# A selective scan on one core: the carried states copied by DMA instead of GpSimd, with three buffers for the scan's output

## The chip, the cores and the metric

The kernel runs on one core of one Trainium2 chip. The metric is the device time of one execution in microseconds. The core's engines are TensorE (PE, with its weight loads shown apart as PEld), VectorE (DVE), ScalarE (ACT), GpSimd (POOL) and SyncE (SP, which here issues nearly all DMAs); sixteen DMA engines move data.

## The reference

Four residual layers on an image batch of 8 × 64 × 64 × 192 in float32, each `x = x + layer(groupnorm(x))`. Layer 0 is a chunked state space block with an MLP, layers 2 and 3 are depthwise convolutions. The change lies in layer 1, a two-dimensional selective scan: the image is read in K = 4 orders (rows, columns, and both backwards), and in each order a recurrence runs over L = 4096 positions for 384 channels with 16 states each:

```
def step(h, inp):
    u_l, d_l, B_l, C_l = inp
    dA = jnp.exp(d_l[..., None] * A)
    dBu = d_l[..., None] * B_l[:, :, None, :] * u_l[..., None]
    h = dA * h + dBu
    y = jnp.sum(h * C_l[:, :, None, :], axis=-1)
    return (h, y)
inputs = (xs, delta, Bs, Cs)          # position first
h0 = jnp.zeros((Bn, 4, Din, N), xs.dtype)
_, ys = jax.lax.scan(step, h0, inputs)
```

Here `delta` is a softplus of a small projection of the input. The four results are put back in image order, added, normalised, gated and projected.

## The kernel before

The program runs layer 0, then layer 1 in three parts (`layer1_in`, `layer1_scan`, `layer1_out`), then layers 2 and 3. The scan part is the long one, and the change is in it.

**Tiling.** The positions lie along the free dimension, 512 (NJ) at a time; the 384 channels are three tiles (o = 0, 1, 2) of 128 partitions. A *piece* is one image b, one order k and one stretch p of 512 positions; there are 8 × 4 × 8 = 256 pieces, listed in `steps`. A piece has 16 states n; one state of one piece is a *group* g of three scans, one for each o. So there are 256 × 16 = 4096 groups and 12,288 scans, numbered j. The pieces of one image and order follow one another, and each needs the last value of every state of the piece before it: these values are kept in the small tile `st` [128 channels, 3, 16 states].

**One scan.** `ahead(j)` computes on ACT `dA = exp(dl * A)` (L1045) and on PE, into a PSUM tile `pd`, the term `delta * u * B` turned to channels by positions (L1051 and L1053). What PE turns is prepared on ACT by `scale` (L1029): for even groups a diagonal matrix `bd` of B, for odd groups the rows `sb` already multiplied. `scan(j)` runs the recurrence on DVE in one instruction (L1086), from `dA`, `pd` and the start value `st[:, o, n]`, into `h`. A tile `h` [128, 3, 512] serves all three scans of a group. GpSimd multiplies `h` by the row C, spread over all partitions in the tile `bc`, giving `hc` (L1095). After the third scan of a group GpSimd copies the last column of `h` (the first one for the backward orders) into `st[:, :, n]` (L1097), for the next piece. `behind(j)` adds `hc`, turned, into the PSUM tile `yt` on PE (L984), summing over the states. When a piece is done, ACT copies `yt` out to `ys` (L999) and SP stores it (L1003).

**Work for the next piece.** `prepare` returns a list of small steps with due times, done between the scans of the present piece: loads of `xt` and `dut` (L923, L925), a turn on PE (L930) and its copy `xs` on ACT (L934), the store of the C rows to DRAM, `bcd` (L936), three projections on PE (L943), the softplus on ACT (L948, L951, L954) and DVE (L957, `dl`), and the four products `dut` on DVE (L970). For k = 0 a further input `uD` is loaded (L1077).

**Order.** The order on PE, DVE, ACT and GpSimd is that in which the program is written (`every_engine`); each engine works strictly in order. The loop at L1111 calls, for each j: `fetch(g + 2)` at o = 0 (the DMA of `bc`, L1035), `ahead(j + 2)`, `scale(g + 2)`, `scan(j)`, `behind(j - 2)`, then the steps that are due. The DMAs on SP are ordered by the framework, and SP too works in order: a DMA that has to wait for an engine holds up the ones behind it. The buffers are `h` 2, `hc` 6, `dA` 5, `pd` 3, `bc` 4, `bd` 10, `sb` 8; a buffer is used again when all its readers are done.

Of the kernel before, what the change touches and what calls it, by code (L numbers as in the profile page):

```python
# [19 lines left out]
DP, DT = 128, 3  # L20
# [5 lines left out]
NJ = 512  # L26
# [3 lines left out]
class Names:  # L30
    n = 0


def mk(pool, shape, tag, **kw):
    Names.n += 1
    return pool.tile(shape, F32, tag=tag, name=f"{tag}_{Names.n}", **kw)
# [837 lines left out]
def layer1_scan(ctx: ExitStack, tc, a, load, ur, ut, xd, yk, cst):  # L874

    nc = tc.nc
# [16 lines left out]
    sp = ctx.enter_context(tc.tile_pool(name="s1", bufs=2))  # L893
# [120 lines left out]
    brows, decay, turned, states, held, outs, sts = {}, {}, {}, {}, {}, {}, {}  # L1014
# [54 lines left out]
    def scan(j):  # L1069
        if not 0 <= j < total:  # L1070
            return
        g, o = divmod(j, DT)
        s, n = divmod(g, N1)
        b, k, p, first = steps[s]
        if k == 0 and n == 5:
            v = ready[s]["u", o] = mk(sp, [DP, NJ], "uD", bufs=DT)
            nc.sync.dma_start(v, ur[b][:, o, p * NJ : (p + 1) * NJ])  # L1077
        if first and n == 0 and o == 0:
            sts[k] = mk(pp, [DP, DT, N1], "st")
        st = sts[k]  # L1080
        rev = slice(None, None, -1) if k >= 2 else slice(None)
        last = 0 if k >= 2 else NJ - 1
        if o == 0:
            states["h"] = mk(sp, [DP, DT, NJ], "h", bufs=2)
        h = states["h"]
        nc.vector.tensor_tensor_scan(  # L1086
            h[:, o, rev],
            decay.pop(j)[:, rev],
            turned.pop(j)[:, rev],
            0.0 if first else st[:, o, n : n + 1],  # L1090
            ALU.mult,
            ALU.add,
        )
        hc = states[j] = mk(sp, [DP, NJ], "hc", bufs=6)
        nc.gpsimd.tensor_tensor(hc, h[:, o, :], held[g], ALU.mult)  # L1095
        if o == DT - 1:
            nc.gpsimd.tensor_copy(st[:, :, n], h[:, :, last])  # L1097

    with every_engine(tc):
        for _, f, *v in prepare(*steps[0][:3], ready[0]):  # L1100
            f(*v)
            if f.__name__ == "turned_xd":
                tc.keep_in_program_order(nc.scalar.preload_act_table_set("natural_log_exp_and_others"))
        fetch(0)
        fetch(1)
        scale(0, range(NB))
        scale(1, range(NB))
        ahead(0)
        ahead(1)
        todo, late = [], []  # L1110
        for j in range(total + 3):  # L1111
            g, o = divmod(j, DT)
            s, i = divmod(j, PER)
            if i == 5 and s + 1 < len(steps):
                todo = prepare(*steps[s + 1][:3], ready[s + 1])
            if o == 0:
                fetch(g + 2)
            ahead(j + 2)
            scale(g + 2, ((0, 1), (2,), (3,))[o])
            while late:  # L1120
                f, *v = late.pop(0)
                f(*v)
            scan(j)
            behind(j - 2)
            while todo and todo[0][0] <= i - 5:
                _, f, *v = todo.pop(0)
                f(*v)
# [190 lines left out]
```

## Time and profile before

| | |
|---|---|
| Runs (three) | 26157.72, 26190.96, 26194.59 us; median 26190.96 |
| Profiled execution, own time | 26178.77 us |
| Its span, first to last instruction | 26177.0 us |
| Busy over the span | PE 23676.9 (90%), PEld 18442.5 (70%), DVE 22201.3 (85%), ACT 20110.8 (77%), POOL 17658.9 (67%) |
| Mean granted TensorE clock | 0.948 over the span, 1.00 in the scan from 14500 to 19500 us |
| DMA, whole span | 1461962 packets, 2275.55 MB, mean 87 GB/s |

The profile is one execution of the program. An engine is busy from an instruction's start to its end; instructions of one engine can overlap, so the sum of durations can be more than the busy time, and starts show the pace better than durations. In the groups of instructions, `hc<-h,bc` means that the tile `hc` is written from `h` and `bc`; then follow the shapes, the count, the busy time with the mean in nanoseconds, and the idle time of the engine just before these instructions, with the one that ended most of it. In the waits, three numbers stand behind a pair: microseconds in total, times, longest. In a timeline the columns are start, duration and engine, instructions of one kind in a row are merged (x3), and what is in brackets is the idle time before, with its releaser. In a line of a stretch, the two first numbers are its bounds, the next its length, then come the busy times of PE, PEld, DVE, ACT and POOL with the counts, the clock, the DMA engines' busy share and GB/s.

### The profile page before, as it was taken

What the parts mean: (1) busy time and instruction counts of PE and PEld (TensorE: products, weight loads), DVE (VectorE), ACT (ScalarE), POOL (GpSimd) and SP (SyncE); (2) the same over time, 40 slices, a digit from 0 to 9 for tenths busy, and PEclk for the clock granted to TensorE, in tenths of its full rate; (3) what the DMA queues carried; (4) which work ended last, traced back from release to release, by engine and by line L of the source; (5) the groups of instructions that cost most, each with busy time, mean ns of one, the idle gap of its engine ahead of it and who ended that gap; (6) DMA issues with size and microseconds to landing.
All of it is one profiled execution on the core that took longest, in us unless ns stands there. A gap on an engine that the chain in (4) does not pass through costs nothing.

```text
span 26177.0 us, 442405 instructions
## 1 busy us (share of the span) xinstructions
PE 23676.9 (90%) x156160; PEld 18442.5 (70%) x156160; DVE 22201.3 (85%) x25001; ACT 20110.8 (77%) x40019; POOL 17658.9 (67%) x18396
## 2 busy tenths in 40 slices
PE   7888888888899999999999999999999999987766
PEld 4444444445588888888888888888888888863322
DVE  6777777756799999999999999999999999986566
ACT  4555555544499999999999999999999999974322
POOL 2222222210199999999999999999999999972100
PEclk8888888889999999999999999999999999998878
DMA  1111111113333333333333333333333333346311
GB/s 56 42 43 42 44 41 44 35 40 115 112 101 94 97 102 94 96 103 94 96 103 94 96 102 95 95 101 96 95 100 97 95 99 97 96 143 198 120 34 29
DMA packets 1461962, 2275.55 MB, mean 87 GB/s; under 512 B 247181, under 2 KB 773133, under 8 KB 1458202
## 3 DMA queue, kind: packets, MB, share of 16 engines
q1 hardware_dynamic: 1445402, 2196.90, 28.9%
q0 software_dynamic: 14336, 50.34, 0.5%
q8 instruction: 1232, 20.19, 0.3%
q14 instruction: 992, 8.13, 0.1%
HBM read 1811.37 MB, written 435.42 MB: 86 GB/s over the span
## 4 chain that ended last, share of the span: by engine, by line
PE 37%; ACT 29%; POOL 13%; DVE 13%; issue 6%; DMA 2%; POOLq 0%; SPq 0%; DVEq 0%; ACTq 0%
ACT dA L1045 12%; POOL hc L1095 10%; PE pd L1051 6%; ACT sb L1029 6%; PE yt L984 5%; DVE h L1086 5%; ACT bd L1029 4%; PE y L643 3%; PE fc L677 3%; DVE x L71 2%; PE pd L1053 2%; DMA yin<-y 2%; PE mm L399 2%; PE mm L943 2%; PE y L576 1%
## 5 line engine op out<-in xcount | busy, mean ns | idle before, releaser
L1095 POOL TENSOR_TENSOR hc<-h,bc 128x512 f32<-128x512 f32 x12288 | 15443.8, 1291 | 477.5 <-DVE h L1086 337.3
L1086 DVE TENSOR_TENSOR_SCAN h<-dA,st,pd 128x512 f32<-128x512 f32 x10752 | 12951.9, 1262 | 533.1 <-PE pd L1051 371.8
L1045 ACT ACTIVATE dA<-dl,A_logs 128x512 f32<-128x512 f32 x12288 | 8785.3, 715 | 46.9 <-DVE h L1086 39.6
L984 PE MATMUL yt<-sq,hc 128*128 128x128 f32 x49152 | 7489.9, 275 | 203.2 <-POOL hc L1095 102.8
L1051 PE MATMUL pd<-bd,dut 128*128 128x128 f32 x49152 | 6581.5, 277 | 254.2 <-DVE h L1086 232.1
L1051 PEld LDWEIGHTS pd<-bd,dut 128*128 128x128 f32 x49152 | 5968.6, 192 | 610.1 <-PE yt L984 342.9
L984 PEld LDWEIGHTS yt<-sq,hc 128*128 128x128 f32 x49152 | 5668.5, 141 | 649.3 <-POOL hc L1095 629.2
L1029 ACT ACTIVATE sb<-dut,xt 128x384 f32<-128x384 f32 x8192 | 4762.6, 606 | 1.1 <-DVE dut L970 1.0
L1053 PE MATMUL pd<-sq,sb 128*128 128x128 f32 x24576 | 3739.6, 275 | 9.3 <-DVE h L1086 0.4
L1053 PEld LDWEIGHTS pd<-sq,sb 128*128 128x128 f32 x24576 | 2821.8, 141 | 480.5 <-DVE dl L957 380.8
L1029 ACT ACTIVATE bd<-sq,xt 128x128 f32<-128x128 f32 x8192 | 3010.2, 392 | 0.0
L1086 DVE TENSOR_TENSOR_SCAN h<-dA,pd 128x512 f32<-128x512 f32 x1536 | 1772.8, 1203 | 115.4 <-PE pd L1051 75.8
L71 DVE SCALAR_TENSOR_TENSOR x<-x,w,x 96x3969 f32<-96x3969 f32 (+1 forms) x192 | 838.3, 4366 | 486.9 <-ACT x L64 483.9
L538 POOL TENSOR_TENSOR xdt<-xb,dtv 128x384 f32<-128x384 f32 x256 | 222.2, 868 | 1366.9 <-ACT xb L532 1366.8
L413 POOL COPY halo<-raw 128x12 f32<-128x12 f32 x64 | 13.0, 202 | 1375.7 <-ACT raw L403 1375.7
L304 DVE SCALAR_TENSOR_TENSOR x<-xs,cpe_w,x 96x504 f32<-96x504 f32 (+1 forms) x1024 | 902.1, 881 | 30.1 <-ACT x L292 20.3
L826 DVE SCALAR_TENSOR_TENSOR u<-xa,conv_w,u 128x504 f32<-128x504 f32 x1152 | 850.0, 742 | 50.2 <-ACT u L818 12.5
L943 PE MATMUL mm<-xs,w_dt 13*128 13x512 f32 x1536 | 863.0, 641 | 1.8 <-DVE dl L957 1.0
L677 PE MATMUL fc<-ff,fc_w 128*96 128x512 f32 x1536 | 861.0, 677 | 2.7 <-DVE xo L680 2.7
L1097 POOL COPY st<-h 128x3 f32<-128x3 f32 x4096 | 831.1, 203 | 0.0
L304 DVE SCALAR_TENSOR_TENSOR xs<-x0h,cpe_w,xs 96x504 f32<-96x504 f32 (+1 forms) x1024 | 757.8, 745 | 23.7 <-ACT xs L292 2.5
L643 PE MATMUL y<-hn,fc_w 96*128 96x512 f32 x1536 | 750.2, 627 | 0.1
(234 smaller groups left out, 25752.7 us busy)
## 6 DMA issues: line engine op xcount, KB each, us to landing
bc<-bcd SPq DMA_DIRECT2D x4096, 256.0 KB
yin<-y SPq DMA_DIRECT2D x256, 768.0 KB
csb<-csd SPq DMA_DIRECT2D x256, 384.0 KB
dut<-ut SPq DMA_DIRECT2D x128, 768.0 KB
y<-ys SPq DMA_DIRECT2D x128, 768.0 KB
dut<-ut SPq DMA_DIRECT2D x256, 384.0 KB
y<-ys SPq DMA_DIRECT2D x256, 384.0 KB
xt<-x1d SPq DMA_DIRECT2D x128, 384.0 KB
```

The lines of the kernel that those rows point to most:

```text
L71: nc.vector.scalar_tensor_tensor(d[:, h0:h1, w0:w1], s[:, h0 + dy : h1 + dy, w0 + dx : w1 + dx], w[:, ct, tap : tap + 1], d[:, h0:h1, w0:w ...
L304: nc.vector.scalar_tensor_tensor(d[:, :, w0:w1], s[:, dy : dy + R, w0 + dx : w1 + dx], w[:, ct, tap : tap + 1], d[:, :, w0:w1], ALU.mult, ...
L643: nc.tensor.matmul(ps, f1w[:, ct, o * 128 : (o + 1) * 128], hn2[q][:, ct, :], start=ct == 0, stop=ct == CT - 1)
L677: nc.tensor.matmul(ps, f2w[:, o, ct * CP : (ct + 1) * CP], ff[:, o, :], start=o == 0, stop=o == 5)
L943: nc.tensor.matmul(ps, w_dt[:, k, o * 128 : (o + 1) * 128], made["xs"][0 : 1 + R1, :], start=True, stop=True)
L984: nc.tensor.matmul(yt[:, t * 128 : (t + 1) * 128], src[:, t * 128 : (t + 1) * 128], mat, is_transpose=mat is ident, start=first and t == 0 ...
L1029: nc.scalar.activation(v, src, AF.Copy, scale=m["xt"][:, t, 1 + R1 + n : 2 + R1 + n])
L1045: nc.scalar.activation(dA, ready[s]["dl"][:, o, :], AF.Exp, scale=aneg[:, k, o, n : n + 1])
L1051: nc.tensor.matmul(dst, ready[s]["dut"][:, t, cols], brows[g, t], start=True, stop=True)
L1053: nc.tensor.transpose(dst, brows[g, t][:, cols], ident)
L1086: nc.vector.tensor_tensor_scan(h[:, o, rev], decay.pop(j)[:, rev], turned.pop(j)[:, rev], 0.0 if first else st[:, o, n : n + 1], ALU.mult, ...
L1095: nc.gpsimd.tensor_tensor(hc, h[:, o, :], held[g], ALU.mult)
```

## The change

The copy of the last column into `st` on GpSimd becomes a DMA issued by SP. It moves one float from each of three columns in each of 128 partitions, so 384 single floats, within SBUF. The tile `h` gets three buffers in place of two. On PE, DVE and ACT the instructions and their order stay the same; GpSimd's list loses the 4096 copies; SP's list gains 4096 DMAs, each ahead of the `bc` fetch for four groups later. The first scan of a group waited, for the `h` buffer, for work of GpSimd two groups back; it now waits for work of GpSimd and for the state DMA of the group three back.

```
@@ def scan(j)
         rev = slice(None, None, -1) if k >= 2 else slice(None)
         last = 0 if k >= 2 else NJ - 1
         if o == 0:
-            states["h"] = mk(sp, [DP, DT, NJ], "h", bufs=2)
+            states["h"] = mk(sp, [DP, DT, NJ], "h", bufs=3)
         h = states["h"]
...
         hc = states[j] = mk(sp, [DP, NJ], "hc", bufs=6)
         nc.gpsimd.tensor_tensor(hc, h[:, o, :], held[g], ALU.mult)
         if o == DT - 1:
-            nc.gpsimd.tensor_copy(st[:, :, n], h[:, :, last])
+            nc.sync.dma_start(st[:, :, n : n + 1], h[:, :, last : last + 1])
```

More of the change, by code (lines that the diff above doesn't have):

```diff
@@ L1083, in scan @@
         if o == 0:
-            states["h"] = mk(sp, [DP, DT, NJ], "h", bufs=2)
+            states["h"] = mk(sp, [DP, DT, NJ], "h", bufs=3)
         h = states["h"]
@@ L1096, in scan @@
         if o == DT - 1:
-            nc.gpsimd.tensor_copy(st[:, :, n], h[:, :, last])
+            nc.sync.dma_start(st[:, :, n : n + 1], h[:, :, last : last + 1])
     with every_engine(tc):
```

## The prediction

> **What bounds the kernel now.** I read the page first (busy times, costliest groups), then the busy times of one 5 ms stretch of the scan, its waits, and the timelines of single engines over one piece.
>
> The page gives the size of what is removed. In the groups (busy us, mean ns; then idle before), the state copy L1097 is a short POOL instruction that follows every third L1095:
>
> ```profile
> L1095 POOL TENSOR_TENSOR hc<-h,bc 128x512 f32<-128x512 f32 x12288 | 15443.8, 1291 | 477.5 <-DVE h L1086 337.3
> ...
> L1097 POOL COPY st<-h 128x3 f32<-128x3 f32 x4096 | 831.1, 203 | 0.0
> ```
>
> The stretch 14500 to 19500 us shows no free engine: of 5000 us PE is busy 4857, DVE 4788, ACT 4883, POOL 4880, and the DMA engines 0.35.
>
> ```profile
> 14500.00:19500.00 5000.00, 4856.81 (x40097) 4425.50 (x40096) 4787.50 (x4344) 4883.23 (x9871) 4879.54 (x5053) 1.00 0.35 98
> ```
>
> A piece (16 states of three scans) takes 62.93 us there: the copies' times repeat at that distance. 5000/62.93 is 79.5 pieces, 1270 groups of three; 256 pieces are the whole stage. Idle per piece: ACT 1.47 us, POOL 1.52, PE 1.80, DVE 2.67.
>
> The waits of the same stretch say what that idle time is. ACT's is nearly all waits for PE (xs and ys); DVE waits for PE's pd; PE waits for POOL's hc; a scan hardly ever waits for POOL, so two h buffers are not short today:
>
> ```profile
> PEld yt L984 <- POOL hc L1095: 191.3, 552, 0.5
> DVE h L1086 <- PE pd L1051: 137.6, 186, 1.3
> ...
> ACT xs L934 <- PE mm L930: 51.7, 79, 0.9
> ACT ys L999 <- PE yt L984: 45.0, 72, 1.3
> ...
> ACT dA L1045 <- DVE h L1086: 10.9, 19, 0.6
> ...
> DVE h L1086 <- POOL hc L1095: 0.4, 1, 0.4
> ```
>
> The timelines show how these hang together. POOL, back to back:
>
> ```profile
> 15005.17 3.76 POOL L1095 TENSOR_TENSOR hc<-h,bc 128x512 f32<-128x512 f32 x3
> 15008.88 0.18 POOL L1097 COPY st<-h 128x3 f32<-128x3 f32 x1
> 15009.03 3.76 POOL L1095 TENSOR_TENSOR hc<-h,bc 128x512 f32<-128x512 f32 x3
> ```
>
> One group takes 3.86 us here (15005.17 to 15009.03; the trace's median is 3.84). Instructions overlap: by the trace's starts, one hc follows another after 1.237 us, and after 1.367 us where a copy lies between. So a copy costs POOL 0.130 us, not the 203 ns of its row. DVE without a stall:
>
> ```profile
> 15001.84 1.28 DVE L1086 TENSOR_TENSOR_SCAN h<-dA,st,pd 128x512 f32<-128x512 f32 x1 [0.26 <-PE pd L1051]
> 15004.32 3.78 DVE L1086 TENSOR_TENSOR_SCAN h<-dA,st,pd 128x512 f32<-128x512 f32 x3 [1.20 <-PE pd L1051]
> ...
> 15035.97 28.56 DVE L1086 TENSOR_TENSOR_SCAN h<-dA,st,pd 128x512 f32<-128x512 f32 x24
> ```
>
> Its starts lie 1.171 us apart, 3.51 per group. For the eight groups in which DVE has only scans, POOL thus falls 0.33 us per group behind it: the start of hc after the end of its scan grows from 0.14 us (group 14 of a piece) to 2.17 (group 5 of the next). PE works in order and takes hc as input, so it comes late too; then PE holds up DVE (0.26 and 1.20 us above, group 6) and ACT:
>
> ```profile
> 14998.62 0.58 ACT L934 COPY xs<-mm 45x512 f32<-45x512 f32 x1 [0.66 <-PE mm L930]
> ```
>
> In groups 6 to 13 ACT's softplus and DVE's dl and dut set the pace; POOL waits there and its backlog vanishes.
>
> **The change part by part.**
>
> *4096 copies leave POOL.* 4096 × 0.130 = 532 us of POOL's path. It isn't all gain. The next engine is ACT with 1.47 us idle per piece: 256 × 1.47 = 376 us is the ceiling as long as ACT does the same work (the change takes none from it). What can be had is ACT's waits that come from POOL's backlog. With copies gone POOL loses 3 × 1.237 − 3.51 = 0.20 us per group in place of 0.33; over the seven steps from group 14 to group 5 the lag ends at 0.14 + 7 × 0.20 = 1.54 in place of 2.17 or more, 0.63 us shorter. ACT's wait for xs falls in group 5 and is 51.7/79 = 0.65 us per piece: nearly all of it goes. Its wait for ys is 45.0/79 = 0.57, in groups 15 and 0, where the lag shrinks from 0.5–0.9 to 0.3–0.5: I take 0.2. Sum 0.85 us per piece, 256 × 0.85 = 218 us. Late next is ACT itself, then PE, which keeps its 0.57 − 0.2 of ys and its own matmuls between pd and yt.
>
> *4096 DMAs come onto SP's queue.* SP's issues in the trace take 0.32 us for 128 rows (bc) and 0.43 for 512 rows of 180 bytes (xt); I take 0.45 for 384 rows. With bc's 0.32 that is some 0.8 us per 3.9 us group, so SP has room. SP now stands at each of them until the third scan is done. Queued behind it: bc for four groups on, and once per piece bcd, xt, dut, y, uD. The order of instructions has bc(g+4) behind st(g); bc(g+4) waits for hc of group g, which itself starts after that scan, so the added wait delays no bc. The others have slack of 10 us and more (xt: issued at 15037.55, turned by PE at about 15061). I put all this at nothing; without that cover, a late bc would stop POOL, one for one.
>
> *The DMA's landing.* It reads h, so the buffer of h is free only when it has landed. By the order of the changed kernel's instructions the first scan of a group waits for the DMA of the group three before it. That is two groups, 7.0 us, after the third scan ended. Between st's issue at that end and the next use lie: 0.45 issue, about 1 us to the first packet (bc issued at 15001.30, first packet at 15002.25), its packets, and what is ahead in the rings (bc: 8 packets × 84 ns per engine = 0.7 us). That leaves 7.0 − 2.2 = 4.8 us for 24 packets per engine. This is what the third buffer pays for: with two, the time would be 3.5 us and the cover 1.3 us. For its own sake the third buffer is worth nothing (0.4 us of waits in 5000).
>
> *What 384 packets of four bytes cost* isn't in the trace of before: no DMA there moves single elements from SBUF to SBUF. The nearest rows: the 180-byte packets of xt take 15 ns each (median), the 24-byte ones of small loads 9 ns, and xt's 512 packets all ran between 15038.94 and 15040.28, 1.34 us. So 24 × 15 = 0.36 us per engine and group beside 0.35 × 3.96 = 1.39 us of other traffic, a share of about 0.45. Against it stands the Trainium skill, "DMA: Bandwidth & Descriptors": under "Rules for kernel authors" a strided last dimension becomes one descriptor per element and transfers under 64 KB are mostly overhead, and under "Measured (HBM→SBUF, 128 partitions, SWDGE, issued from GpSimd)" it counts about 10.5 ns per packet of the transfer, not of the engine. By that, 384 packets take an estimated 4.0 us, longer than a group, and with the other 1.39 the DMA engines would set 5.4 us per group: 1.46 × 4096 = 6 ms more. The row is from this chip's own queue and has 512 packets in 1.34 us, so I follow it: cost nothing, bounds 0 and +6 ms. It can't be below zero: the DMA takes nothing away but the copy, counted above.
>
> Sum against the profiled execution: its own time 26178.8 us (span 26177.0) − 218 = 25961; the median of the runs, 26191, is 12 us above it, so 25973. I say 25970.
>
> **The rivals.**
>
> *ACT's waits go altogether.* For: with POOL below DVE's stalls PE is earlier everywhere, and 107.6 of ACT's 116.8 idle us are waits for others. Gain 1.3 to 1.47 us per piece, 330 to 376 us: about 25840.
>
> *PE holds it where it is.* For: PE is busy 4857 of 5000, and DVE's stall of 1.20 us ends on pd right after a 1.12 us matmul (L943) in PE's own order, not on hc. Then xs and ys wait as before and the gain is at most 0.2 us per piece: 26140 to 26191. Against: PE's weight loads wait 191.3 us for hc in this stretch, the longest of all waits.
>
> *The state DMA lands late (the slower side).* Place: the first scan of a group, waiting for the DMA three groups back. It decides from a landing over 7.0 us after the third scan's end, that is from 4.8 us / 24 = 200 ns per packet in quiet stretches, and earlier in the 7 us of each piece in which xt, dut and y keep the DMA engines 50 to 80% busy. Two waits of half a microsecond per piece there: 256 × 1.0 = 256 us more, 26450. Against: 15 ns per packet in the nearest row. Beyond 107 ns per packet (24 × 107 ns + 1.39 = 3.96) the DMA engines are the bound in every group and it is far worse.
>
> **How the numbers follow.** 0.2% is 52 us, about what a measurement of this kernel can tell from no change. Forecast (25900 to 26080) 0.48; ACT's waits gone 0.17; PE holds it 0.15; late landing 0.20. Faster is the first two, 0.65; same is the third, 0.15; slower the last, 0.20. The range, 25830 to 26240, takes in the first three and the mild edge of the last.
>
> **What would show it.** L1097 gone from POOL, and hc's starts 1.237 us apart throughout; ACT's wait for xs from 0.65 to below 0.2 us per piece; DVE's stall in group 6 shorter; DMA share in the scan 0.40 to 0.50; a piece near 62.1 us. I am wrong if DVE's h shows waits for a DMA, if st's packets take far over 15 ns, or if ACT waits for PE as long as before though POOL is earlier.

## The result and the profile after

The changed kernel takes 25995.07 us (median of four runs, 25988.56 to 26014.83); the kernel before, run beside it, 26182.07. The ratio is 0.9931, with a 95% interval of [0.9914, 0.9948]: 187 us or 0.7% faster. The profiled execution took 25998.18 us, against 26178.77 before, which is 180.6 us less. The stage from the first scan to the last hc shrank by 180.1 us (16217.7 to 16037.5 in the traces), so all of it lies in the scan.

The page's groups. L1097 is gone from POOL. The idle time ahead of hc rose from 477.5 to 814.5 us: a part of what the copies gave back is now waiting.

```profile
L1095 POOL TENSOR_TENSOR hc<-h,bc 128x512 f32<-128x512 f32 x12288 | 15304.6, 1287 | 814.5 <-DVE h L1086 358.3
L1086 DVE TENSOR_TENSOR_SCAN h<-dA,st,pd 128x512 f32<-128x512 f32 x10752 | 12878.6, 1260 | 447.0 <-PE pd L1051 311.0
```

The stretch from 14500 to 19500 us (bounds, length, busy PE, PEld, DVE, ACT, POOL, clock, DMA share, GB/s). POOL falls from 4880 to 4770 busy us although it does 1% more hc; the other engines do more in the same 5 ms; the DMA share rises from 0.35 to 0.41:

```profile
14500.00:19500.00 5000.00, 4877.35 (x40551) 4476.67 (x40550) 4813.68 (x4388) 4930.62 (x9973) 4770.31 (x3831) 1.00 0.41 99
```

Its waits (us in total, times, longest):

```profile
PEld yt L984 <- POOL hc L1095: 119.1, 330, 0.4
DVE h L1086 <- PE pd L1051: 117.6, 120, 1.3
...
ACT ys L999 <- PE yt L984: 46.6, 73, 1.3
...
ACT dA L1045 <- DVE h L1086: 12.2, 21, 0.6
...
PE yt L984 <- POOL hc L1095: 4.0, 26, 0.2
...
ACT xs L934 <- PE mm L930: 1.2, 5, 0.3
```

For hc, PE has one line in the waits as PEld and one as PE; the second read, before:

```profile
PE yt L984 <- POOL hc L1095: 31.1, 133, 0.3
```

PE's waits for hc fell from 191.3 + 31.1 to 119.1 + 4.0, DVE's waits for L1051 from 137.6 to 117.6 us (186 to 120 times), ACT's wait for xs from 51.7 to 1.2. ACT's wait for ys stayed. DVE's scans wait for no DMA in this stretch. The timeline of DVE over one piece shows a part of what went: before, group 6 had two stalls, 0.26 and 1.20 us; now the first is gone and the second is as long as it was.

```profile
15011.11 29.44 DVE L1086 TENSOR_TENSOR_SCAN h<-dA,st,pd 128x512 f32<-128x512 f32 x25
15041.75 3.78 DVE L1086 TENSOR_TENSOR_SCAN h<-dA,st,pd 128x512 f32<-128x512 f32 x3 [1.20 <-PE pd L1051]
```

From the starts of hc in the traces one gets the pace by groups of a piece (means over k = 1 to 3, the last piece of each order left out; us), and the lag, which is hc's start after the end of its scan, at the last scan of group 5 (median):

| kernel | groups 14, 15, 0 to 6 | groups 7 to 13 | piece | lag |
|---|---|---|---|---|
| before | 34.57 | 28.27 | 62.84 | 2.23 |
| changed | 33.41 | 28.74 | 62.15 | 1.75 |

In nine groups POOL works without a pause and gains 1.16 us, which is 9 × 0.13. In the other seven it used to work off its lag; now it arrives earlier and waits there, and 0.47 us is given back. What is left is 0.69 us per piece, 177 us in 256 pieces.

The starts of DVE's scans tell where in the piece the time went (means over the same pieces). From the last scan of group 3 to the first of group 6, DVE took 9.01 us before and takes 8.35 now: 0.66 of the 0.69 us lies there, where POOL's lag is largest. The stall of 0.26 us is its largest part; the rest are gaps so short that the timeline merges them into its rows.

### The profile page after: what moved, and what is told of

Read it like the earlier page. It is cut to its first block, busy times and chain, and to the rows that moved or that the text cites. A ratio compares the mean times of both kernels' runs of the same rounds, so it can differ in the third digit from the quotient of the medians.

```text
span 25996.4 us, 448176 instructions
## 1 busy us (share of the span) xinstructions
PE 23556.4 (91%) x156160; PEld 18440.5 (71%) x156160; DVE 22125.1 (85%) x25001; ACT 20098.7 (77%) x40019; POOL 17143.5 (66%) x14300
## 2 busy tenths in 40 slices
DMA packets 3100407, 2282.47 MB, mean 88 GB/s; under 512 B 1885581, under 2 KB 2411533, under 8 KB 3096602
## 4 chain that ended last, share of the span: by engine, by line
ACT 42%; PE 38%; DVE 11%; POOL 3%; issue 3%; DMA 2%; SPq 0%; POOLq 0%; DVEq 0%; ACTq 0%
ACT dA L1045 18%; ACT sb L1029 10%; PE pd L1051 7%; PE yt L984 6%; ACT bd L1029 6%; DVE h L1086 3%; PE y L643 3%; PE fc L677 3%; DVE x L71 2%; DMA yin<-y 2%; PE mm L399 2%; PE pd L1053 2%; POOL hc L1095 2%; ACT ys L999 1%; PE y L576 1%
## 5 line engine op out<-in xcount | busy, mean ns | idle before, releaser
L1095 POOL TENSOR_TENSOR hc<-h,bc 128x512 f32<-128x512 f32 x12288 | 15304.6, 1287 | 814.5 <-DVE h L1086 358.3
L1051 PE MATMUL pd<-bd,dut 128*128 128x128 f32 x49152 | 6581.3, 277 | 253.5 <-DVE h L1086 231.3
L1051 PEld LDWEIGHTS pd<-bd,dut 128*128 128x128 f32 x49152 | 5968.4, 192 | 609.4 <-PE yt L984 342.2
```

What stands on the lines that cost most here:

```text
L1051: nc.tensor.matmul(dst, ready[s]["dut"][:, t, cols], brows[g, t], start=True, stop=True)
```

## The experiments

Ten kernels were run, in three sets on three chips: the first four, the next four, and the last two. Each set had the kernel before beside it on the same chip; ratios are to that kernel, with their 95% intervals, and kernels of different sets are compared by these ratios alone.

**Three buffers alone.** The kernel before with

```
-            states["h"] = mk(sp, [DP, DT, NJ], "h", bufs=2)
+            states["h"] = mk(sp, [DP, DT, NJ], "h", bufs=3)
```

> The kernel before with three buffers for h, the copies still on GpSimd. Theory (the gain is GpSimd's 0.130 us per group, which reaches the end through ACT's wait for xs): no change from before, 26160 to 26200 us, since scans waited for GpSimd only 0.4 us in 5 ms. Rival (the third buffer lets the scans run further ahead and gives part of the 187 us): 26000 to 26130.

Measured: 26192.18 us, ratio 1.0007 [0.9999, 1.0015]. The third buffer gives nothing by itself; the rival falls.

**The DMA with two buffers.** The changed kernel with `bufs=2` for h.

> The changed kernel with two buffers for h. Theory (the third buffer is the cover of the DMA's landing): in the changed kernel's trace the state DMA lands 2.3 us after its issue in the median and over 4.3 us in one case of ten, and one landing in five comes later than the first scan two groups on. So scans wait for the DMA, 0.5 to 2 us per piece after what GpSimd's backlog absorbs: 26120 to 26500, at or above the kernel before. Rival (landings are quick enough, the third buffer does nothing): 25980 to 26020.

Measured: 26426.32 us, ratio 1.0094 [1.0080, 1.0107]. So it is 0.9% slower than before, and 1.6% slower than with three buffers (1.0094/0.9931). In its waits over the same stretch DVE now waits for the DMA:

```profile
DVE h L1086 <- DMA st<-h: 82.9, 97, 2.6
DVE h L1086 <- PE pd L1051: 64.3, 126, 1.6
```

and its timeline shows one such wait, and one for POOL's hc, in the groups that ran without a gap in the changed kernel:

```profile
15014.37 7.13 DVE L1086 TENSOR_TENSOR_SCAN h<-dA,st,pd 128x512 f32<-128x512 f32 x6
15022.43 10.65 DVE L1086 TENSOR_TENSOR_SCAN h<-dA,st,pd 128x512 f32<-128x512 f32 x9 [0.93 <-DMA st<-h]
15033.78 11.82 DVE L1086 TENSOR_TENSOR_SCAN h<-dA,st,pd 128x512 f32<-128x512 f32 x10 [0.70 <-POOL hc L1095]
```

The third buffer is the cover of the DMA's landing; a piece takes 63.97 us without it (measured as in the table above).

**No state kept.** The changed kernel without the DMA:

```
         if first and n == 0 and o == 0:
             sts[k] = mk(pp, [DP, DT, N1], "st")
+            nc.gpsimd.memset(sts[k], 0.0)
...
-            nc.sync.dma_start(st[:, :, n : n + 1], h[:, :, last : last + 1])
+            pass
```

> The changed kernel without the state DMA: the last columns are not kept, st is set to zero once per image and order, and every piece after the first starts from zero. Three buffers for h. Theory (the DMA costs nothing): the same as the changed kernel, 25970 to 26010. Rival (the DMAs' packets, issues or landings cost part of what the copies gave back): 25800 to 25950.

Measured: 25993.79 us, ratio 0.9931 [0.9918, 0.9943], the changed kernel's own ratio. 4096 DMAs behind three buffers cost nothing that can be measured; the rival falls.

**ACT's xs copy one scan later.** The kernel before with

```
-        at = [(0, fetch_rows), (8, turn_xd), (9, turned_xd)]
+        at = [(0, fetch_rows), (8, turn_xd), (10, turned_xd)]
```

> The kernel before, with the copies on GpSimd and two h buffers; only the due time of ACT's copy of xs is 10 in place of 9, one scan later. Theory (the gain goes through ACT's wait for xs, 0.65 us per piece): that wait goes here too, and with it 0.4 to 0.65 us per piece, 100 to 166 us: 26010 to 26080. Rival (the wait is a symptom and GpSimd's own path sets the time of a piece): 26150 to 26200.

Measured: 26172.81 us, ratio 1.0002 [0.9993, 1.0010]. No gain, but the run doesn't decide: ACT's wait was not taken away, it went to the next thing that ACT wants from PE:

```profile
ACT e L948 <- PE mm L943: 67.4, 79, 1.1
ACT ys L999 <- PE yt L984: 45.0, 72, 1.3
```

My theory that the gain goes through ACT's wait for xs was now in doubt. I formed another: POOL's lag reaches the end through PE's order. `ahead(j + 2)` stands ahead of `behind(j - 2)` in each turn of the loop, so PE must turn hc(j − 5) before it makes the pd of scan j. As long as POOL's lag is below a limit PE finds hc ready; above it PE waits, and the next scans wait for PE. In the kernel before, POOL's lag would by my estimate grow to some 0.14 + 8 × 0.33 = 2.8 us in group 6, but the trace has it level off at 2.2: the rest, so the theory, is passed on to DVE.

**The DMA in the nine groups only.** The changed kernel with

```
         if o == DT - 1:
-            nc.sync.dma_start(st[:, :, n : n + 1], h[:, :, last : last + 1])
+            if 7 <= n <= 13:
+                nc.gpsimd.tensor_copy(st[:, :, n], h[:, :, last])
+            else:
+                nc.sync.dma_start(st[:, :, n : n + 1], h[:, :, last : last + 1])
```

> The changed kernel with the state DMA only in groups 14, 15 and 0 to 6 of a piece (9 of 16), where GpSimd falls behind the scans; in groups 7 to 13 GpSimd copies as before. Theory (only GpSimd's lag in those groups reaches the end, and only what it has over about 2.2 us): the whole gain, 25975 to 26015 us. Rival (every copy counts alike): 9/16 of 187 us, about 26077.

Measured: 26002.69 us, ratio 0.9932 [0.9920, 0.9945]: the whole gain, with 9 copies of 16 removed. DVE takes 8.36 us from the last scan of group 3 to the first of group 6, as in the changed kernel.

**The DMA in the other seven groups.** The same edit with the condition `not 7 <= n <= 13`.

> The counterpart: the state DMA in groups 7 to 13 (7 of 16), GpSimd's copies in groups 14, 15 and 0 to 6; three buffers for h. Theory (in groups 7 to 13 GpSimd waits for others anyway): no gain, 26160 to 26200 us. Rival (every copy counts alike): 7/16 of 187 us, about 26100.

Measured: 26190.40 us, ratio 1.0007 [0.9998, 1.0016]: nothing, although 1792 copies are gone and POOL's busy time in the stretch is 80 us below that of before:

```profile
14500.00:19500.00 5000.00, 4852.18 (x40056) 4421.09 (x40056) 4787.76 (x4340) 4879.50 (x9862) 4799.18 (x4496) 1.00 0.37 98
```

Copies don't count alike; where they stand decides. DVE's 9.01 us from group 3 to group 6 stay as they were, at 8.99.

**The softplus later.** The kernel before with

```
-        at = [(0, fetch_rows), (8, turn_xd), (9, turned_xd)]
+        at = [(0, fetch_rows), (8, turn_xd), (10, turned_xd)]
...
-            at += [(11 + 4 * o, step_mm, o), (12 + 4 * o, step_abs, o), (13 + 4 * o, step_exp, o)]
-            at += [(14 + 4 * o, step_ln, o), (16 + 4 * o, step_add, o)]
+            at += [(11 + 4 * o, step_mm, o), (14 + 4 * o, step_abs, o), (15 + 4 * o, step_exp, o)]
+            at += [(16 + 4 * o, step_ln, o), (18 + 4 * o, step_add, o)]
...
-            at += [(26 + 3 * t, turn, t), (27 + 3 * t, turned, t)]
+            at += [(28 + 3 * t, turn, t), (29 + 3 * t, turned, t)]
```

> The kernel before, copies on GpSimd and two h buffers, with the xs copy one scan later (10) and, other than with that copy alone, the softplus steps on ACT and DVE and the turns of dut two scans later each. With xs alone ACT's wait for PE only went over to the first softplus step (67.4 us in 5 ms in place of 51.7 at xs), so that run didn't take the wait away. Theory ACT (GpSimd's lag reaches the end through ACT's wait): no such wait is left, 26010 to 26080 us. Theory DVE (it reaches the end through PE's pd, for which the scans wait): 26150 to 26200, the waits of DVE for pd in groups 2 to 6 as before.

Measured: 26195.32 us, ratio 1.0009 [1.0000, 1.0018]. ACT no longer waits for PE at xs or at the softplus, yet nothing is gained; the wait came back at ys (115.5 us in place of 45.0). Theory ACT asked for 26010 to 26080 us and falls, as far as this run can tell. Theory DVE had the time right, but the waits for pd didn't stay as they were: some of them were now put down to ACT's dA:

```profile
ACT ys L999 <- PE yt L984: 115.5, 79, 1.7
DVE h L1086 <- ACT dA L1045: 94.4, 90, 1.3
DVE h L1086 <- PE pd L1053: 75.9, 147, 1.0
DVE h L1086 <- PE pd L1051: 44.6, 102, 1.2
```

So this run speaks against ACT, and alone it doesn't prove PE.

**ACT's ys copy later.** The changed kernel, the copies of yt taken one scan later (the loop runs one turn longer):

```
-            late.append((take, s, o, outs.pop((s, o))))
+            late.append((j + 4, take, s, o, outs.pop((s, o))))
...
-            while late:
-                f, *v = late.pop(0)
+            while late and late[0][0] <= j:
+                _, f, *v = late.pop(0)
```

> The changed kernel with ACT's copy of yt to ys one scan later, which leaves nothing out. ACT waits there for PE 46.6 us in 5 ms, 0.58 us per piece, the one wait of ACT that the prediction had taken for GpSimd's and that stayed. Theory (ACT's idle time is what bounds a piece): up to 0.58 us per piece, 148 us, 25850 to 25900. Rival (in groups 15 and 0 ACT has time to spare, since it runs ahead until its dA buffers are full): no change from the changed kernel, 25980 to 26010.

Measured: 26004.27 us, ratio 0.9934 [0.9921, 0.9946], as the changed kernel. ACT's wait went from ys back to xs:

```profile
ACT xs L934 <- PE mm L930: 51.3, 73, 1.2
...
ACT ys L999 <- PE yt L984: 8.2, 21, 0.4
```

The changed kernel with ACT's xs wait back at its old size is no slower. By these runs that wait is time which ACT has to spare, and it shows up wherever ACT first needs PE.

**PE turns hc later, copies kept.** The test of the new theory: the kernel before with (and the loop one turn longer)

```
-            behind(j - 2)
+            behind(j - 3)
```

> The kernel before, copies on GpSimd and two h buffers, with one edit: PE turns hc into yt one scan later in its order (three scans behind in place of two), so PE asks GpSimd for hc one scan of 1.17 us later. Nothing is left out. Theory (GpSimd's lag reaches the end where PE, in order, waits for hc ahead of the pd that the next scans need, from a lag of about 2.2 us on): the limit rises to about 3.3 us, the lag of 2.8 at the end of the nine groups stays below it, and the gain of the change, some 180 us, comes without touching the copies: 25900 to 26010. Rival (GpSimd's own time over a piece sets the pace, whatever PE does): 26150 to 26200.

Measured: 25978.73 us, ratio 0.9931 [0.9919, 0.9944]: a gain as large as the change's, with every copy still on GpSimd and two h buffers. In the timelines POOL is as slow as before, 3.84 us per group:

```profile
15001.25 3.79 POOL L1095 TENSOR_TENSOR hc<-h,bc 128x512 f32<-128x512 f32 x3
15004.94 0.23 POOL L1097 COPY st<-h 128x3 f32<-128x3 f32 x1
15005.09 3.80 POOL L1095 TENSOR_TENSOR hc<-h,bc 128x512 f32<-128x512 f32 x3
```

but PE hardly waits for it any more (PEld for hc 31.0 us in place of 191.3), and DVE's stalls in group 6 are 0.18 and 0.36 us in place of 0.26 and 1.20:

```profile
PEld yt L984 <- POOL hc L1095: 31.0, 108, 0.4
...
DVE h L1086 <- POOL st L1097: 16.2, 72, 0.4
```

```profile
15016.74 1.28 DVE L1086 TENSOR_TENSOR_SCAN h<-dA,st,pd 128x512 f32<-128x512 f32 x1 [0.18 <-POOL st L1097]
15018.39 3.82 DVE L1086 TENSOR_TENSOR_SCAN h<-dA,st,pd 128x512 f32<-128x512 f32 x3 [0.36 <-PE pd L1051]
```

The 0.18 is the wait for an h buffer: at this lag (2.54 us) the two buffers do become short, and they cost DVE 16.2 us of waits in the stretch.

That the sums agree is in part chance, since the two kernels don't gain in the same places. By the starts of the scans (k = 1 to 3), DVE's 9.01 us from the last scan of group 3 to the first of group 6, where the change saves 0.66, fall by 0.47 here, with POOL no faster. That is the theory's share. The stall of 1.20 us, which the change left alone, falls by 0.83 us, and 0.66 us is given back up to group 10. Pieces of k = 0 gain 1.26 us each (the change: 0.69) and those of k = 1 to 3 gain 0.59 (the change: 0.70), means over all of them.

**The same in the changed kernel.**

> The changed kernel (state DMA, three h buffers) with the same edit, PE turns hc one scan later. Theory (with the copies gone the lag is 1.8 us, already below the limit): little more, at most PE's last wait for hc in group 6, 0.31 us per piece or 80 us: 25900 to 26000, and within 0.3% of the kernel before with this edit. Rival (GpSimd's own time counts): the full difference between the two kernels stays, about 187 us.

Measured: 25962.73 us, ratio 0.9925 [0.9912, 0.9939], 16 us below the run before it. With PE's order loosened, the copies and the third buffer together are worth 16 us and not 187; which of the two brings the 16 wasn't tried, and by the starts of the scans they lie in the pieces of k = 0, while those of k = 1 to 3 take as long as in the run before. It is the fastest kernel of the study, though its interval overlaps that of the changed kernel. The table with four of these runs (k = 1 to 3, as above):

| kernel | groups 14, 15, 0 to 6 | groups 7 to 13 | piece | lag |
|---|---|---|---|---|
| DMA in the nine groups | 33.38 | 28.77 | 62.15 | 1.73 |
| DMA in the other seven | 34.53 | 28.37 | 62.90 | 2.23 |
| before, PE turns later | 34.55 | 27.70 | 62.25 | 2.54 |
| changed, PE turns later | 33.38 | 28.87 | 62.25 | 1.73 |

The third row is the clearest: POOL's nine groups take as long as before, and the piece is shorter, because DVE was held up less and POOL catches up in the other seven. The lag passes 2.2 us, and the one wait for POOL that DVE's timeline then shows is that for an h buffer.

## Why the prediction was right, and where not

*The copy's cost on POOL, 0.130 us per group.* Right: hc's starts lie 1.237 us apart in the nine groups, and a group takes 3.71 us in place of 3.84 (medians).

*The lag at the end of the stretch, 1.54 us in place of 2.17.* Right in kind: 1.63 at the first scan of group 5, the place of these figures (1.75 at the last, where before had 2.23). The lag started higher than I took it, at 0.23 in group 14 in place of 0.14; the growth of 0.20 per group was right.

*0.65 us per piece from ACT's wait for xs, 0.2 from ys.* The mis-sized term is ys: 0.2 forecast, nothing measured (45.0 before, 46.6 after). The xs wait fell from 0.65 to 0.01 us, and the gain is 0.69 us per piece. But that the number fits does not make ACT the way: the wait at xs happened to be as long as what DVE got back between groups 3 and 6 (0.66 us), and that the total came out near is luck in this respect. Waits at xs can be taken off or put back without any effect on the time (the two runs with later ACT copies, and the later softplus). I read them as a second sign of the same thing, PE coming late behind hc. The way that the time takes, by the runs, is POOL's lag, PE's order, pd, the next scans: copies count only where the lag grows, the time comes back in DVE's scans at the end of that stretch, and most of it comes back there too when only PE's order is changed. The prediction had named that chain for DVE and then counted it at ACT.

*ACT as the ceiling, 376 us, and late next.* Not shown: when ACT's waits were moved, the time stayed. ACT is busy 4931 of 5000 us now, but DVE's stall of 1.20 us in group 6 remains as well. In the changed kernel the later turn of hc took 0.87 us off that stall, and 0.99 us was given back up to group 10 (k = 1 to 3). What bounds a piece at 62.2 us was not settled.

*DMA costs nothing, three buffers cover the landing.* Right, and shown from both sides (no state kept, two buffers). The page has 3,100,407 packets in place of 1,461,962, which is 4096 × 400 more, 384 of data and 16 of semaphores each; by the trace the four-byte packets took 9 ns in the median, not 15. The cover of 4.8 us holds for the median alone: st lands 2.3 us after its issue in the median, but later than 4.7 in one case of twenty and 6.8 at worst. The smallest time from landing to the next use was 0.12 us, at one scan of the whole run that did wait; with two buffers, scans that wait start 0.12 us after the landing too. SP's issue took 0.60 us, where I had 0.45. (A group is 62.93/16 = 3.93 us, where I had 3.96; nothing hangs on it.)

*The rule of the Trainium skill* ("DMA: Bandwidth & Descriptors", "Measured (HBM→SBUF, 128 partitions, SWDGE, issued from GpSimd)"), by which, in my estimate, 384 packets would have taken 4.0 us and the DMA engines set 5.4 us per group: the measurement decides against it for this queue. The whole DMA lands in 2.3 us in the median, the DMA share is 0.41, and leaving the DMAs out changes nothing.

*The rivals.* ACT's waits did not go altogether: ys stayed. PE holding it where it is did not come, but its reading of the stall of 1.20 us was right: the stall in group 6 that got shorter is only the first one. The late landing came only where the third buffer was taken away. There it made the kernel 255 us slower than before and 1.6% slower than the changed kernel; I had put 256 us on it with three buffers, so that likeness is chance.

## What to carry to other kernels

Here an engine that fell behind cost nothing until its lag reached the look-ahead of another engine that works in order and needs its output. First look for that limit, since one step later in one engine's order was worth as much as 4096 copies removed. Long waits of a busy engine don't yet show that the time goes through it: move one and see whether the time moves or only the wait. Two changes with the same gain need not gain in the same place, so compare the starts of the scans and not only the sums. When a copy becomes a DMA, its source buffer has to outlive the landing, so count the buffers against the late landings (here 4.7 to 6.8 us) and not against the median (2.3).

## What was not expected of the hardware

SP's issues slowed down behind two stores in a row. After the two stores of y (384 KB each), the next state DMA took 1.64 us to issue and the bc fetch behind it 1.48, where 0.60 and 0.33 are usual (changed kernel, start and duration):

```profile
15024.26 1.27 SPq L1003 DMA_DIRECT2D y<-ys  x2
15025.62 1.64 SPq L1097 DMA_DIRECT2D st<-h  x1
15027.56 1.48 SPq L1035 DMA_DIRECT2D bc<-bcd  x1
15029.13 0.61 SPq L1097 DMA_DIRECT2D st<-h  x1
```

In 109 of the 128 pieces with two stores of y the state DMA behind them took over 1 us to issue; behind the single store of 768 KB in the other pieces it took 0.60 in the median. The groups behind still had their data in time: in the whole run bc landed at least 5.3 us before its first use. What makes the issue slow was not tried.
